# Four-layer graph network: comparisons moved to VectorE, and three steps reordered across the engine queues

## The chip, the cores and the metric

The kernel runs on one core of a Trainium2 chip. The metric is the device time of one execution in microseconds (us), here the median of several runs. A core has five engines that run side by side and meet through semaphores: PE (TensorE, matrix products), DVE (VectorE), ACT (ScalarE), POOL (GpSimd) and SP, which in this kernel issues nearly all of the DMA transfers. PEld is TensorE's weight load.

## What is computed

The input `x` is 32 x 512 x 128 (32 batches, 512 nodes, 128 features) and `adj` is 512 x 512, about one eighth of it non-zero. Four layers follow each other, each of the form `x = x + layer(relu(layernorm(x)))`:

```python
# layer 0: attention whose scores are table values placed at adj's non-zero entries in row-major order
m   = adj > 0
idx = cumsum(m.reshape(-1)) - 1                  # an index beyond the 256 entries takes the last
A   = softmax(where(m, e[0][idx], -9e15), axis=1)
out = (A * I) @ (h @ W[0]) + (A * (1 - I)) @ (h @ W[1]) + bias
# layer 1: Chebyshev hops over adj, one product with Theta1, relu
# layer 2: relu(h @ psi); weights adj * adj; a two-layer perceptron of the messages and h
# layer 3: tanh-limited attention masked by adj, then @ x @ v
```

Products are in float32; the kernel splits their operands into three parts ("high", "low", "mid") and adds three products where it needs the precision.

## The kernel before

**The order is the source's order.** The whole body lies in `tc.manual_schedule(...)`: on PE, DVE, ACT and POOL the instructions stand as the Python statements issue them, and DMA issues marked `keep_in_program_order` stand so on SP. Each engine takes its instructions in order, so one that waits holds back all behind it. Many helpers are Python generators: `go(steps, n)` advances one by n steps, `next(steps)` by one. That is how pieces of later work are placed between pieces of earlier work.

**Tiles.** The 32 batches are 16 pairs (`NQ`), and 512 nodes are 4 row blocks (`NT`). A pair's `h` (normalised and rectified) is 8 tiles of 128x128 made by ACT on L313. Its statistics are four DVE instructions `bn_stats` and then small operations that give `sh` and `rs`. For pairs 0, 1 and 2 these are POOL's (L233 to L237, `early_stats`); for later pairs ACT takes the root (L255), DVE the inverse (L257) and POOL the shift (L259, L260).

**Turned h.** The products need `h` with features on the partitions. Pairs 0 to 2 are turned by PE (L596, L331) and copied by ACT. All others go by memory (`turn_steps`): DVE transposes in 32x32 blocks into `hb` (L349), SP issues four writes (L356), then one read (L358) brings `hT` back. In layer 2 and later `turn_half` (L1101, L1107) and `fetch` (L1115) do the same.

**The opening of layer 0** builds the softmax matrix from `adj`.
1. `m`, its row counts and their running sums `incl` and `before` are formed.
2. For each row block t, `lt` (L554) compares a row of numbers with `incl`, and `of_row` (L555) marks which table entries lie in that row block. PE sums over them (`p_row`, `p_known`).
3. ACT and DVE copy `pgs`; PE forms `p_upto`; DVE compares and counts (L616), which gives each entry's column `col_of`.
4. `at_row` and `at_col` (L619, L620) mark rows and columns; `at_part` (L624) marks the column with one of three parts of the table's value, for two groups `kk` of 128 entries: six operations of 128x512.
5. `score_rows(t)` has PE add these up into `p_later` (L656) and `p_val` (L660); `softmax_rows(t)` is two DVE operations (L667, L669) and ACT's exponential (L670); `scaled_rows(t)` divides (row 0 on POOL, L678; others on ACT, L680) and POOL takes the diagonal out (L683, L684).
6. The rows are turned by PE (L485) and split by ACT and DVE into `att_high`, `att_low`, `att_mid` (L376 to L390), a half at a time.

`project_first(b)` makes the three parts of `g`, pair 0's product with W[1]: PE (L446), `g_high` (ACT L638 for b = 0, DVE L636 for b = 1), `g_low` (DVE, L640), `g_mid` (POOL, L641).

**The rounds of layer 0.** `first_sums()` handles pair 0 and prepares pairs 1 to 4; `round0(q)` handles pair q. A round of PE is 16 matmuls with the diagonal's operand `hd` (L796), 16 of the next pair's projection `p_g` (L446), and 48 with att and `g` (L803): high, low and mid parts for each half I. `diagonal_of(q, b)` makes `hd` on POOL (L731) from turned h; `bias(q)` adds the layer's bias to x on POOL (L453); `g_high`, `g_low` and `g_mid` are on ACT (L468), DVE (L470) and POOL (L474). DVE adds the sums to x (L811).

**Layer 1** is one generator, `layer1`, driven as `next_layer`: its first steps are interleaved with the last rounds of layer 0. `straighten(q)` (POOL, L936) reorders turned h into `hs`; `split_up` and `split_turned` form three parts of `h` and `hs` (ACT L412, POOL L413, DVE L414); `first` is the product with adj (`p_x1T`, L397), `weighed` the products with Theta1 (`p_w`, L962 and L964), `mix` the second product with adj (`p_l`, L983), whose sums DVE finishes (L987, L989) and to whose `hs` POOL adds the bias (L977).

**Layer 2** begins inside the last round of layer 1 by way of `more(step)`, with steps 5 to 8 after the four final `mix` calls. `split_hT(n)` splits turned h of batch n (POOL L1150 and L1151, DVE L1153), `opened(n)` makes the first products with it (`p_feat` L1163, `p_hidden` L1166).

The places that the change touches, in this order, are the loop with L554, the two `go(normal[0], ...)` beside the pgs copies, the loop with L624, the sequence from `project` to `transpose_rows`, the end of `first_sums`, the middle of `round0`, the head of `layer1`, steps 4 and 5 of `more`, and the loop at the end of the body.

Of the kernel before, what the change touches and what calls it, by code (L numbers as in the profile page):

```python
# [29 lines left out]
def kernel(  # L30
# [520 lines left out]
    pg = [bank(f"p_row_{i}").rearrange("p (j k) -> p j k", j=2) for i in range(NT // 2)]  # L551
    for t in range(NT):
        s = prep.tile([P, NE], F16, tag="lt", name=f"lt_{t}", bufs=2)
        (nc.gpsimd if t in (1, 2) else nc.vector).tensor_scalar(s, cols[:, :NE], incl[:, t : t + 1], None, OP.is_lt)  # L554
        nc.vector.scalar_tensor_tensor(of_row[:, t, :], cols[:, :NE], before[:, t : t + 1], s,  # L555
                                       OP.is_ge, OP.mult)
        for j in range(NT):
            nc.tensor.matmul(pg[j // 2][:, j % 2, :], m[:, t, blk(j)], of_row[:, t, :],
                             start=(t == 0 and j % 2 == 0), stop=(t == NT - 1), skip_group_check=True)
# [3 lines left out]
    for kk in range(NK):  # L563
        for t in range(NT):
            nc.tensor.matmul(pb[:, kk, :], of_row[:, t, blk(kk)], known[:, t, :],
                             start=(t == 0), stop=(t == NT - 1))
    go(normal[0], 1)
    pgs = prep.tile([P, NT, NE], F16, name="pgs")
    nc.scalar.copy(pgs[:, 0:2, :], pg[0])
    nc.vector.tensor_copy(pgs[:, 2:4, :], pg[1])  # L570
# [1 line left out]
    nc.vector.tensor_copy(row_of, pb[:, :, 1])  # L572
    rest = prep.tile([P, NK], F32, name="rest")
    nc.vector.tensor_sub(rest, rows[:, :NK], pb[:, :, 0])
    go(normal[0], NT - 1)

    elastn = prep.tile([P, 1], F32, name="elastn")
    nc.gpsimd.tensor_scalar(elastn, elast, -1.0, None, OP.mult)
# [41 lines left out]
        nc.vector.tensor_scalar(at_col[:, kk, :], cols, col_of[:, kk : kk + 1], -1.0, OP.is_equal, OP.mult)  # L620
    for kk in range(NK):
        for i in range(3):
            eng = nc.gpsimd if kk and i else nc.vector
            eng.tensor_scalar(at_part[:, i, kk, :], cols, col_of[:, kk : kk + 1],  # L624
                              parts[i][:, kk : kk + 1], OP.is_equal, OP.mult)
    copies = [None, nc.scalar.copy, nc.scalar.copy]
    turned = [q and pe_steps(h[q], f"hT0_{q}", hT[q], copies[q]) for q in range(3)]
    g_tiles(0)
# [14 lines left out]
    project = [[project_first(b) for b in range(2)], project_steps(1, hT[1])]  # L643
    next(project[0][0])
    go(normal[0])
    go(project[0][0])


    diag = prep.tile([P, NT, P], F32, name="diag")
# [35 lines left out]

    squares = turn_adj()
    score_rows(0)
    softmax_rows(0)
    score_rows(1)
    go(early[1], 1)  # L690
    turn_first(1)
# [9 lines left out]
    go(early[1], 1)  # L701
    next(project[0][1])
    softmax_rows(3, lambda: inverse(2))
    go(early[1])
    scaled_rows(2)
    next(project[0][1])
    inverse(3)
    scaled_rows(3)
    pt = [bank(f"p_attT_{j}") for j in range(NT)]
    transpose_rows(pt, att, 0)  # L710
    transpose_rows(pt, att, 1)
# [101 lines left out]
    def first_sums():  # L813


        adiag.append(region0.tile([P, N], F32, name="adiag", bufs=1))
        ps = opened_sums(0)
        mixed(0, 0, ps[0], 0, True)
        transpose_rows(pt, att, 2)
        transpose_rows(pt, att, 3)  # L820
        for j in range(NT):
            att_high(j, 1, True)
        go(normal[1])
        go(early[2])
        att_low(1)
        att_mid(1)
        mixed(0, 0, ps[0], 1, True)
        mixed(0, 0, ps[0], 2, True)
        p_adiag = bank("p_adiag")
        for t in range(NT):  # L830
            nc.tensor.matmul(p_adiag[:, blk(t)], ones, diag[:, t, :], start=True, stop=True)
        nc.scalar.copy(adiag[0], p_adiag)
        diagonal_of(0, 0)
        diagonal_of(0, 1)
        next(turned[1])
        mixed(0, 1, ps[1], 0, True)
        go(turned[1])
        next(project[1])
        mixed(0, 1, ps[1], 1, True)
        mixed(0, 1, ps[1], 2, True)  # L840
        go(project[1])
        go(normal[2])
        own_sums(0, ps, False)
        diagonal_of(1, 0)
        diagonal_of(1, 1)
        go(ln3, NT + 1)
        for I in range(2):
            added(0, I, ps[I])
        next(turned[2])
        go(turned[2])  # L850
        go(ln3)
        normalise(3)
        go(ahead[4], NT + 1)
        go(turn(3))
        go(ahead[4])
        bias(0)

    def round0(q):

        more = q + 1 < NQ  # L860
        nothing = iter(())
        both = stats_of_two(q - 1, q + 5) if q + 5 < NQ else stats_steps(q - 1, apart=True)
        ps = opened_sums(q)
        own_sums(q, ps, True)
        if q == 1:
            normalise(4)
            go(ahead[5])
        elif q + 3 < NQ:
            go(turn(q + 3))
        if q + 4 < NQ:  # L870
            h[q + 4] = normed_tile(q + 4)
            normal_of = normed_steps(q + 4, h[q + 4])
        else:
            normal_of = nothing
        if q > 1:
            go(normal_of, NT)
        go(both, NT)
        if q == NQ - 1:
            next(next_layer)
        if more:  # L880
            diagonal_of(q + 1, 0)
            diagonal_of(q + 1, 1)
            steps = projection(q + 1)
            next(steps)
            bias(q + 1)
            go(steps)
        if q + 5 >= NQ:
            go(both)
        if q == 1:
            go(turn(4))  # L890
        go(normal_of)
        if q >= 5:
            go(sums_ahead, 1)
        for part in range(3):
            mixed(q, 0, ps[0], part, False)
        go(both, NT + 1)
        added(q, 0, ps[0])
        go(both)
        if q in (3, 4):
            next(squares)  # L900
            next(squares)
        if q == 5:
            go(squares)
        for part in range(3):
            mixed(q, 1, ps[1], part, False)
        added(q, 1, ps[1])
        if q == NQ - 1:
            own[q] = stats_steps(q)
        if q % 2 and q // 2 + NQ // 4 < NQ // 2:
            loads(q // 2 + NQ // 4)  # L910

    def layer1(more, square):
# [80 lines left out]
        turn(0)  # L993
        normalised(1)
        yield
        pair = small_tile("th_high", F32R), small_tile("th_low", F32R)
        th_parts = pair[0][:, : 2 * D], pair[0][:, 2 * D :], pair[1][:, : 2 * D]
        fixed_parts(th[:, 0:2, :].rearrange("p k f -> p (k f)"), *th_parts)
        split_up(0, 0)
        turn(1)  # L1000
        split_up(0, 1)
        split_up(1, 0)
        normalised(2)
# [435 lines left out]
    def more(step):  # L1439

        if step == 0:
            chunk(2, 0)
            chunk(2, 1)
        elif step == 1:
            turn_half(2, 0)
        elif step == 2:
            turn_half(2, 1)
            fetch(2, 0)
            entering["weights"] = weights_of_2()
            next(entering["weights"])  # L1450
        elif step == "weights":
            go(entering["weights"])
        elif step == 3:
            entering["split"] = steps_of_split(0)
            next(entering["split"])
        elif step == 4:
            chunk(2, 2)
            chunk(2, 3)
            go(entering["split"])
        elif step == 5:  # L1460
            turn_half(2, 2)
            opened(0)
            turn_half(2, 3)
            fetch(2, 1)
            split_hT(1)
        elif step == 6:
            weighed_by_phi(0)
            chunk(2, 4)
        elif step == 7:
            turn_half(2, 4)  # L1470
            chunk(2, 5)
        elif step == 8:
            turn_half(2, 5)
            chunk(2, 6)
# [2 lines left out]
    first_sums()  # L1477
    bias(1)
    for q in range(1, NQ):
        if q == NQ - 2:  # L1480
            next(next_layer)
        round0(q)
    own_scope.close()
# [38 lines left out]
```

## Time and profile before

| | |
|---|---|
| median of 3 runs | 897.44 us (895.27 to 898.77) |
| the profiled execution | 897.51 us, of which 895.7 us are its span (first to last instruction) |
| busy, share of the span | PE 98%, PEld 86%, DVE 79%, POOL 69%, ACT 64% |
| mean granted TensorE clock | 0.994 |
| DMA moved | 103.90 MB, mean 116 GB/s |
| PE busy in 0 to 20, 20 to 40, 40 to 60 us | 13.59, 16.75, 17.06 us |
| PE busy in 80 to 100 and 100 to 120 us | 20.00 and 20.00 us |

Times inside the execution are counted from the start of its span. A row of the profile names the line of the source, the engine, the operation, output <- inputs, shapes and the number of instructions. "Idle before, releaser" is how long the engine stood idle ahead of that instruction and what ended the idleness. Idle time of an engine that nobody waits for costs nothing. L313 stands for `h` in layers 0 and 1, L1092 for it in layers 2 and 3.

### The profile page before, as it was taken

To read this page: it belongs to the slowest core of one execution; us is meant where nothing else is said; L and a number is where in the kernel's file an instruction comes from. 1 tells how busy PE (TensorE), PEld (TensorE's weight loads), DVE (VectorE), ACT (ScalarE), POOL (GpSimd) and SP (SyncE) were. 2 spreads that over 40 slices of the span, in tenths; PEclk is the share of its full clock that TensorE was granted. 3 is DMA by queue.
4 is the path that set the end of the run, shared out by engine and by line. 5 is a ranking of instruction groups with operands and counts; after the bars stand their busy time and mean duration, and the time that the engine had idled before them with its cause. 6 is when DMAs were issued, how large, how long until landed. Compare 5 with 4: busy or idle time off the path is not lost.

```text
span 895.7 us, 16285 instructions
## 1 busy us (share of the span) xinstructions
PE 874.1 (98%) x5519; PEld 773.2 (86%) x5520; DVE 703.9 (79%) x1424; ACT 574.9 (64%) x1278; POOL 617.7 (69%) x629
## 2 busy tenths in 40 slices
PE   6989999999999999999999999999999999999998
PEld 3789999997888888888878888888888889999987
DVE  6778787557778777797678888888779898988875
ACT  3675555246555556555666888885688878766774
POOL 7678888848578777666867557666376766676664
PEclk9989999999999999999999999999999999999999
DMA  9128663222231222213143345455345555555432
GB/s 259 27 71 236 189 185 100 70 71 72 82 106 48 71 71 68 74 48 95 48 142 95 95 119 141 126 157 165 110 139 152 150 146 152 143 153 147 127 104 83
DMA packets 107683, 103.90 MB, mean 116 GB/s; under 512 B 9552, under 2 KB 94160, under 8 KB 107600
## 3 DMA queue, kind: packets, MB, share of 16 engines
q1 hardware_dynamic: 107312, 102.34, 40.6%
q8 instruction: 44, 0.72, 0.3%
q10 hardware_dynamic: 288, 0.52, 0.2%
q14 instruction: 39, 0.32, 0.1%
HBM read 53.02 MB, written 49.81 MB: 115 GB/s over the span
## 4 chain that ended last, share of the span: by engine, by line
PE 87%; POOL 6%; ACT 2%; issue 1%; DVE 1%; DMA 1%; SPq 0%; POOLq 0%; ACTq 0%; DVEq 0%
PE p_av L1290 12%; PE p_hidden L1186 10%; PE p_l L803 9%; PE p_score L1268 9%; PE p_l L983 9%; PE p_x1T L397 9%; PE p_w L962 5%; PE p_l L446 3%; PE p_z L446 3%; PE p_l L796 3%; PE p_g L446 3%; PE p_w L964 3%; PE p_query L1222 2%; PE p_feat L1163 2%; PE p_hidden L1166 2%; PE p_hv L1234 2%
## 5 line engine op out<-in xcount | busy, mean ns | idle before, releaser
L1290 PEld LDWEIGHTS p_av<-hv,ex 128*128 128x128 f32 x1024 | 119.1, 191 | 4.0 <-POOL hv L1252 1.0
L1290 PE MATMUL p_av<-hv,ex 128*128 128x129 f32 x1024 | 119.7, 274 | 0.8 <-POOL hv L1252 0.6
L313 ACT ACTIVATE h<-x,sh,rs 128x128 f32<-128x128 f32 x256 | 103.3, 483 | 17.6 <-POOL sh L282 10.1
L427 POOL TENSOR_TENSOR key<-key 128x512 fp32r<-128x512 f32 x32 | 47.9, 1496 | 84.1 <-DVE key L426 58.2
L1263 DVE TENSOR_TENSOR ex<-ex,adjTx 128x512 f32<-128x512 f32 x64 | 80.4, 1259 | 31.1 <-ACT ex L1261 29.6
L1263 POOL TENSOR_TENSOR ex<-ex,adjTx 128x512 f32<-128x512 f32 x64 | 99.6, 1574 | 6.9 <-issue 3.5
L1092 ACT ACTIVATE h<-x,sh,rs 128x128 f32<-128x128 f32 x256 | 102.9, 484 | 0.0
L413 POOL TENSOR_TENSOR low_h<-h,high_h 128x512 fp32r<-128x512 f32 x32 | 55.6, 1739 | 44.9 <-PE p_w L964 32.5
L1269 ACT ACTIVATE ex<-p_score 128x512 f32<-128x512 f32 x128 | 76.3, 598 | 11.5 <-PE p_score L1268 4.7
L1261 ACT ACTIVATE ex<-ex 128x512 f32<-128x512 f32 x128 | 77.3, 634 | 0.0
L1150 POOL TENSOR_SCALAR high_hT<-hT 128x512 fp32r<-128x512 f32 x32 | 20.5, 642 | 57.4 <-PE p_hidden L1166 26.6
L246 DVE BATCH_NORM_STATS2 bn<-x 128x6 f32<-128x256 f32 x160 | 58.2, 418 | 0.0
L1206 POOL TENSOR_TENSOR x<-x,phi2b 128x256 f32<-128x256 f32 x64 | 55.7, 890 | 0.0
L413 POOL TENSOR_TENSOR low_hs<-hs,high_hs 128x512 fp32r<-128x512 f32 x32 | 44.1, 1388 | 15.7 <-ACT high_hs L412 15.3
L399 ACT COPY x1T<-p_x1T 128x512 f32<-128x512 f32 x32 | 18.7, 586 | 56.1 <-PE p_x1T L397 56.1
L1268 PE MATMUL p_score<-high_query,key 128*128 128x512 f32 x128 | 50.6, 395 | 0.0
L1268 PE MATMUL p_score<-low_query,key 128*128 128x512 f32 x128 | 50.5, 394 | 0.0
L1268 PE MATMUL p_score<-mid_query,key 128*128 128x512 f32 x128 | 50.4, 394 | 0.0
L431 ACT ACTIVATE high_query<-p_query 128x512 fp32r<-128x512 f32 x32 | 19.2, 601 | 47.5 <-PE p_query L1222 47.5
L964 PE MATMUL p_w<-th,x1T 128*128 128x128 f32 x256 | 49.0, 272 | 0.0
L962 PE MATMUL p_w<-th_high,high_hs 128*128 128x256 f32 x128 | 45.4, 355 | 0.1
L1151 POOL TENSOR_TENSOR low_hT<-hT,high_hT 128x512 fp32r<-128x512 f32 x32 | 42.5, 1328 | 4.3 <-POOL high_hT L1150 2.3
(249 smaller groups left out, 2619.5 us busy)
## 6 DMA issues: line engine op xcount, KB each, us to landing
d<-hb SPq DMA_DIRECT2D x128, 128.0 KB, 2.4
hT<-d SPq DMA_DIRECT2D x32, 512.0 KB, 3.7
d_hT<-hb_hT SPq DMA_DIRECT2D x116, 128.0 KB, 2.4
hT<-d_hT SPq DMA_DIRECT2D x29, 512.0 KB, 3.3
x<-in_x_dram SPq DMA_DIRECT2D x32, 256.0 KB, 5.1
dv<-hvb SPq DMA_DIRECT2D x128, 64.0 KB, 1.9
hvt<-dv SPq DMA_DIRECT2D x32, 256.0 KB, 2.7
out_dram<-x SPq DMA_DIRECT2D x31, 256.0 KB, 2.5
```

The lines of the kernel that those rows point to most:

```text
L313: nc.scalar.activation(h[:, b, t, :], xt[q][:, b, t, :], AF.Relu, bias=shift[q][:, i : i + 1], scale=scale[q][:, i : i + 1])
L397: nc.tensor.matmul(p, right[part][:, blk(t)], left[part][:, t, :], start=(t == 0 and part == 0), stop=(t == NT - 1 and part == 2))
L413: nc.gpsimd.tensor_sub(low, x, high.bitcast(F32))
L446: nc.tensor.matmul(p[:, blk(t)], hT(t), w, start=(i == 0), stop=(i == len(terms) - 1))
L803: nc.tensor.matmul(p[:, i * 2 * D : (i + 1) * 2 * D], att_parts[part][:, t, blk(2 * I + i)], g[q][part][:, t].rearrange("p b f -> p (b f)" ...
L962: nc.tensor.matmul(p, hs_parts[q, b][part][:, blk(t)], th_parts[part], start=(part == 0 and t % 2 == 0), stop=False, skip_group_check=True)
L983: nc.tensor.matmul(p, adj_parts[part][:, t, blk(i)], w[r][part][:, t, :], start=(part == 0 and t == 0), stop=(part == 2 and t == NT - 1))
L1092: nc.scalar.activation(h[:, t, :], xt[q][:, b, t, :], AF.Relu, bias=shift[q][:, i : i + 1], scale=scale[q][:, i : i + 1])
L1186: nc.tensor.matmul(sums2[n], weighed_features[n][i][:, blk(t)], sq[i][:, t, :], start=False, stop=(i == 2 and t == NT - 1), skip_group_che ...
L1263: eng.tensor_mul(split(ex[:, t, :]), split(ex[:, t, :]), crossed(mask[:, t, :]))
L1268: nc.tensor.matmul(p, keys[n][i][:, t, :], query[n][i], start=(i == 0), stop=(i == 2))
L1290: nc.tensor.matmul(po[:, i, : D + 1], ex[:, t, blk(i0 + i)], hv[:, t, :], start=(t == 0), stop=(t == NT - 1))
```

## The change

Five edits; no arithmetic is added or removed.

1. `lt` of row blocks 1 and 2 (L554) and `at_part` of group 1, parts 1 and 2 (L624), four instructions, go from POOL to DVE. Two of pair 0's h tiles, not one, stand ahead of ACT's pgs copy.
2. The second and third step of pair 0's `project_first(0)` stand after row 0's scores and softmax; on DVE this puts `g_low` behind row 0's two softmax operations.
3. The last steps of pair 1's early statistics (four POOL operations) stand after row 3's diagonal, not between the diagonals of rows 1 and 2.
4. `diagonal_of(2, ...)` (two POOL operations) is issued at the end of `first_sums`, ahead of `bias(0)` and `bias(1)`, not in round 1 behind them and pair 5's shift.
5. Layer 1's first two steps are each taken one or two rounds sooner: h of pair 0 in round 13, its transposes and transfers with h of pair 1 in round 14, and the transposes and transfers of pair 1 in round 15. In layer 2 the transposes of batches 2 and 3 and the read of their turned h come in step 4, before the last four `mix` calls, not in step 5.

```diff
-        (nc.gpsimd if t in (1, 2) else nc.vector).tensor_scalar(s, cols[:, :NE], incl[:, t : t + 1], None, OP.is_lt)
+        nc.vector.tensor_scalar(s, cols[:, :NE], incl[:, t : t + 1], None, OP.is_lt)
...
-    go(normal[0], 1)
+    go(normal[0], 2)
     pgs = prep.tile([P, NT, NE], F16, name="pgs")
...
-    go(normal[0], NT - 1)
+    go(normal[0], NT - 2)
...
         for i in range(3):
-            eng = nc.gpsimd if kk and i else nc.vector
-            eng.tensor_scalar(at_part[:, i, kk, :], cols, col_of[:, kk : kk + 1],
-                              parts[i][:, kk : kk + 1], OP.is_equal, OP.mult)
+            nc.vector.tensor_scalar(at_part[:, i, kk, :], cols, col_of[:, kk : kk + 1],
+                                    parts[i][:, kk : kk + 1], OP.is_equal, OP.mult)
...
     next(project[0][0])
     go(normal[0])
-    go(project[0][0])
...
     score_rows(0)
+    next(project[0][0])
     softmax_rows(0)
+    go(project[0][0])
     score_rows(1)
...
     softmax_rows(3, lambda: inverse(2))
-    go(early[1])
     scaled_rows(2)
     next(project[0][1])
     inverse(3)
     scaled_rows(3)
+    go(early[1])
     pt = [bank(f"p_attT_{j}") for j in range(NT)]
...
         go(ahead[4])
+        diagonal_of(2, 0)
+        diagonal_of(2, 1)
         bias(0)
...
-        if q == NQ - 1:
-            next(next_layer)
         if more:
-            diagonal_of(q + 1, 0)
-            diagonal_of(q + 1, 1)
+            if q > 1:
+                diagonal_of(q + 1, 0)
+                diagonal_of(q + 1, 1)
             steps = projection(q + 1)
...
         turn(0)
         normalised(1)
         yield
+        turn(1)
+        yield
         pair = small_tile("th_high", F32R), small_tile("th_low", F32R)
...
         split_up(0, 0)
-        turn(1)
         split_up(0, 1)
...
             go(entering["split"])
-        elif step == 5:
             turn_half(2, 2)
-            opened(0)
             turn_half(2, 3)
             fetch(2, 1)
+        elif step == 5:
+            opened(0)
             split_hT(1)
...
     for q in range(1, NQ):
-        if q == NQ - 2:
+        if q >= NQ - 3:
             next(next_layer)
         round0(q)
```

## The prediction

> **What bounds the kernel now.** I read the page first, then what TensorE waited for, then the time line of each engine where it waits. On the page, row PE is the busy share in 40 slices of 22.4 us, PEclk the granted clock.
>
> ```profile
> PE   6989999999999999999999999999999999999998
> PEclk9989999999999999999999999999999999999999
> ```
>
> From the fourth slice on PE is the bound, and only less PE work or a removed PE stall can shorten that part. The opening, to about 67 us, is not PE-bound: idle time, and one slice at reduced clock. TensorE's waits say where (total us, times, longest):
>
> ```profile
> PE p_l L796 <- POOL hd L731: 3.8, 2, 3.4
> PE p_val L660 <- POOL at_part L624: 3.2, 2, 1.7
> ...
> PE p_w L962 <- POOL low_hs L413: 1.7, 2, 1.5
> ...
> PE p_feat L1163 <- POOL low_hT L1151: 1.3, 1, 1.3
> ```
>
> POOL ends all four, and the change aims at just these. In the time lines (start, length):
>
> ```profile
> 17.67 4.56 POOL L624 TENSOR_SCALAR at_part<-cols,col_of,part 128x512 bf16<-128x512 f16 x2
> 32.09 1.67 POOL L236 TENSOR_TENSOR rs<-sd,minus_half 128x8 f32<-128x8 f32 x1
> 53.67 5.03 POOL L453 TENSOR_TENSOR x<-x,b 128x512 f32<-128x512 f32 x4
> 59.15 2.50 POOL L731 TENSOR_TENSOR hd<-hT,adiag 128x512 f32<-128x512 f32 x2
> 60.47 0.80 PE L796 MATMUL p_l<-w,hd 128*128 128x128 f32 x2 [3.41 <-POOL hd L731]
> 61.70 3.35 PE L796 MATMUL p_l<-w,hd 128*128 128x128 f32 x14 [0.43 <-POOL hd L731]
> ```
>
> See that hd of pair 2 stands behind 5.03 us of biases, and that 14 matmuls then take 3.35 us where sixteen take 1.95 elsewhere. The windows tell why (length, PE busy, clock, DMA):
>
> ```profile
> 57.00:60.40 3.40, 0.06 (x1) 1.00 0.48 154
> 60.40:63.80 3.40, 2.90 (x12) 0.50 0.33 74
> 63.80:67.20 3.40, 3.40 (x18) 0.50 0.30 85
> ```
>
> The stall is followed by 6.8 us at half clock.
>
> **The Trainium skill.** "TensorE: Matmul & The Clock Gate", section "What's actually happening": half rate after an idle window of about 3.4 us, full rate again after a busy one. The windows agree; 0.06 us busy of 3.4 was idle enough. "GPSIMD Engine Reference", section "4.1 Engine selection": elementwise work belongs on VectorE, though one-input operations run at roughly line rate on GpSimd. The trace is harsher: at_part takes 2281 ns on POOL and 407 on DVE, lt 966 and 278. "SBUF — State Buffer", section "SBUF: two separate sides": GpSimd and a VectorE operation with two SBUF inputs exclude each other. Partly so here: one of_row (L555) took 703 ns beside POOL's lt, the others 483 to 490.
>
> **Part 1, comparisons on DVE.** L554: DVE gains two of 278 ns, but it had waited 0.23 and 0.21 us for POOL's: even. POOL loses 1.92 us, so pair 0's first statistics, 10.35 to 12.68, can run from 8.3 to about 10.6 (port conflicts with of_row may cost either side up to 0.7, the range of this step). ACT now does two h tiles (0.41 each) before the pgs copy; both fit before p_row ends at 12.15, so the copy starts at 12.2, not 13.11. p_upto starts at 12.7, not 13.73; DVE's L616, behind its two bn (13.6), at 13.6, not 14.49: 0.9 earlier. L624: six at_part at a pitch of 0.33 on DVE, from 16.89 - 0.9 = 16.0 to 16.0 + 5 x 0.33 + 0.41 = 18.05. POOL delivered its second at 22.24. So p_val of row 0 ends at 18.5, not 22.66, and DVE's L669 starts at 18.6, not 22.69. DVE then bounds the softmax: TENSOR_TENSOR_REDUCE, g_low, one bn, u (0.62 + 0.61 + 0.34 + 0.66), then for row 1 0.62 + 0.07 + 0.67 + 0.66, for row 2 0.62 + 0.07 + 0.33 + 0.65 and an inverse of 0.1: 6.1 us, so row 3's L669 at 24.7, not 30.17. g_low of pair 0 (moved behind row 0's softmax) costs DVE nothing new. ACT's last exp and two scalings end at 27.5.
>
> **Part 2, pair 1's statistics behind row 3.** Four POOL operations, 31.59 to 34.04, 2.45 us. Without them between, row 3's diagonal ends at 29.0, not 35.95; they run 29.1 to 31.5. PE turns rows 2 and 3 by 29.75 and ends the low products at 30.7. What is late next: g_mid of pair 0 (L641, queued behind the statistics) ends at 32.85, so PE waits 2.2 us; and ACT's four h of pair 1 wait for 31.5 with att_high's second half queued behind them. ACT then needs 1.65 + 1.22 + 1.65 to 35.9, adiag 0.5, first turned copy 36.95; p_g of pair 1 starts at 37.0, not 41.21. **The opening gains 4.2 us.** Left in place, the statistics would end at 28.7 and row 3 at 30.65; I take the move alone as -1 to +1.
>
> **Part 3, pair 2's diagonals before the biases.** From p_g of pair 1 the chain is ACT in series (g_high, eight h, table load, sd, turned copies, eight h, sd, then DVE's rs and POOL's sh): sh of pair 4 at 53.72 - 4.2 = 49.5. hd of pair 2 at 49.5 + 2.5 = 52.0; PE ends pair 1's products at 57.06 - 4.2 = 52.85. No stall, no half clock. But three things come due:
> - Turned h of pair 3: DVE's transpose ends at 53.27, its read lands at 60.54; minus 4.2 that is 56.35. PE's own sums end at 54.65: it waits 1.7, then p_g to 58.2, high and low products to 60.1.
> - g_mid of pair 2: 52.0 + biases 5.0 + sh of pair 5 0.5 + bias 2 2.5 + 1.3 = 61.3. PE waits 1.25; the mid products start at 61.35, not 69.67: **8.3 us earlier**, the part before included.
> - Queued behind the biases as well: sh of pair 5 (57.5, was 59.19), eight h, DVE's statistics of pair 0 (they need bias 0, at 54.5), hd of pair 3 (64.4, needed at 65.2), turned h of pairs 4 and 5, which SP issues in order with the x loads (about 67.0 and 75.7; needed 67.0 and 76.4). The cover is thin: another 0 to 1.5 us.
> Later POOL needs 2.5 + 2.5 + 1.3 + 0.5 = 6.8 us a round against PE's 9.33, and recovers.
>
> **Part 4, layer 1.** ACT's eight h of pair 0 (3.18 us) move into round 13, where ACT idles 7.72 before L468; DVE's transposes (1.29 per pair) into the ends of rounds 13 and 14, into idle of over 2 us; eight writes and two reads go on an SP queue that is empty there. So hs (L936), held until 200.86 by the transfer, starts when POOL's low_h ends, 197.8. low_hs of both halves ends by 203; p_w needs the first at 202. The wait of 1.47 and 0.13 ahead of it go: 1.6 us. The waits of 0.16 and 0.23 further on stay.
>
> **Part 5, layer 2.** The second turned h waited at DVE (446.12) behind a sum that POOL's bias (L977) held until 445.05. ACT's h is ready at 441.95; transposed by 442.65, with the same 8.5 us to its landing (447.4 to 455.9), it is there at 451.2, not 456.04. The wait of 1.29 goes. The sum behind it starts 0.1 later, hidden by POOL's hs until 445.05.
>
> **Sum.** 8.3 + 1.6 + 1.3 = 11.2 us off the profiled execution (897.51; span 895.7 to 884.5), which lies 0.07 above the median of the runs shown (897.44): 886.2. If no stall in Part 3 came (bound from below), 3 us more: 883; with 0.7 of conflicts, 1 for Part 2, 1.5 of thin cover and half of Parts 4 and 5 lost, 891.
>
> **The rivals.**
> - *The feeders take part of it back* (0.24). One new PE idle stretch of 1.7 to 2.2 us meets the clock windows badly, one or two windows at half clock (1.7 us each), or the thin cover breaks. For it: three new stalls. Against: none is the 3.4 us of before, and the stretch 12.6 to 16.0 had PE busy only from 13.73 to 15.66 and full clock after it. 889 to 892.9.
> - *The opening's gain is handed back in rounds 2 to 5* (0.06). hd's wait only becomes a wait for turned h or g_mid of the same length, since neither transfers nor biases got shorter. Then Parts 4 and 5 remain: 897.4 - 2.9 = 894.5. Against: turned h lands 4.5 us before PE used it.
> - *Slower* (0.04). One mechanism: in rounds 1 to 3 PE, fed in pieces, falls to half clock again and again. A window of 3.41 us costs 1.7, so the 11.2 are gone from seven windows, 0.5% lost from ten: about 903. Against: at half clock PE needs 18.7 us a round, its feeders catch up, and full windows release it.
> - That the change doesn't act is excluded: the engines' instruction orders of the two kernels differ as the parts say.
>
> **How the numbers follow.** My forecast has 0.66: 882.5 to 889, most likely 886.2. With the first rival the range is 882 to 892. About 0.5%, 4.5 us, is what a measurement can tell from no change. Faster by more: 0.66 + 0.24 - 0.01 = 0.89; within: 0.06 + 0.01 = 0.07; slower: 0.04.
>
> **Right or wrong.** Right: no wait for at_part; L669 of row 0 near 18.6; p_g of pair 1 near 37; hd of pair 2 ready before PE; full clock from 52 to 68; no wait for low_hs of 1.5 nor for low_hT; POOL's third high_hT near 441 in the new time. Wrong: half clock after 52 us, a wait over 3 us for g_mid, hd or hT in rounds 2 to 5, a start of round 2's mid products later than 64.

## The result and the profile after

The changed kernel takes **886.18 us** (median of 4 runs, 885.88 to 886.49) against 896.49 (895.27 to 898.77, 4 runs) for the kernel before: a ratio of 0.9882, 95% interval 0.9860 to 0.9905. The forecast was 886.2. The profiled execution took 886.07 us with a span of 884.3, where the prediction had 884.5.

The two rows of the page, 40 slices of 22.1 us:

```profile
PE   8889999999999999999999999999999999999998
PEclk9999999999999999999999999999999999999999
```

The clock's 8 in the third slice is gone. What TensorE waited for, from the view of its waits (total us, times, longest), the main ones of layer 0 from 14 us on:

```profile
PE p_g L446 <- DMA hT<-d_hT: 1.7, 1, 1.7
PE p_attT L485 <- POOL att L682: 1.3, 1, 1.3
PE p_l L803 <- POOL g_mid L474: 1.0, 1, 1.0
PE p_attT L485 <- POOL sh L234: 0.7, 1, 0.7
...
PE p_g L446 <- DVE x L811: 0.5, 1, 0.5
PE p_l L803 <- POOL g_mid L640: 0.5, 1, 0.5
```

Of the four waits shown of before, those for hd, at_part and low_hT are gone and that for low_hs is down to 0.2. Two of the new ones (1.7 for turned h, 1.0 for g_mid) are those that the prediction named. The time lines of VectorE, GpSimd and TensorE at the places shown of before (start, length, and in brackets the idle time ahead with what ended it):

```profile
15.45 2.02 DVE L623 TENSOR_SCALAR at_part<-cols,col_of,part 128x512 bf16<-128x512 f16 x6
...
29.61 1.67 POOL L236 TENSOR_TENSOR rs<-sd,minus_half 128x8 f32<-128x8 f32 x1
...
49.48 2.54 POOL L731 TENSOR_TENSOR hd<-hT,adiag 128x512 f32<-128x512 f32 x2
51.98 4.98 POOL L453 TENSOR_TENSOR x<-x,b 128x512 f32<-128x512 f32 x4
...
52.72 1.95 PE L796 MATMUL p_l<-w,hd 128*128 128x128 f32 x16
56.33 2.02 PE L446 MATMUL p_g<-w,hT 128*128 128x128 f32 x16 [1.67 <-DMA hT<-d_hT]
...
61.23 1.21 PE L803 MATMUL p_l<-g_mid,att_mid 128*128 128x256 f32 x8 [0.96 <-POOL g_mid L474]
```

Six at_part take 2.02 us on VectorE, where two of them took 4.56 on GpSimd. hd of pair 2 now stands ahead of the biases, is ready at 52.02, and its sixteen matmuls take 1.95 us in one piece. The windows around them (length, PE busy with its number of matmuls, clock, DMA share, GB/s) show the clock at 1.00 throughout:

```profile
57.00:60.40 3.40, 3.27 (x29) 1.00 0.34 75
60.40:63.80 3.40, 2.58 (x21) 1.00 0.48 114
63.80:67.20 3.40, 3.40 (x32) 1.00 0.95 306
```

### The profile page after: what moved, and what is told of

Same layout as the page of the kernel before. It is cut to its first block, busy times and chain, and to the rows that moved or that the text cites. A ratio compares the mean times of both kernels' runs of the same rounds, so it can differ in the third digit from the quotient of the medians.

```text
span 884.3 us, 16285 instructions
## 1 busy us (share of the span) xinstructions
PE 869.4 (98%) x5520; PEld 769.9 (87%) x5520; DVE 704.2 (80%) x1428; ACT 574.3 (65%) x1278; POOL 610.8 (69%) x625
## 4 chain that ended last, share of the span: by engine, by line
PE 89%; DVE 4%; POOL 3%; ACT 2%; issue 1%; DMA 0%; POOLq 0%; DVEq 0%; ACTq 0%
PE p_av L1292 13%; PE p_l L984 10%; PE p_hidden L1188 10%; PE p_x1T L397 10%; PE p_score L1270 9%; PE p_l L803 8%; PE p_w L963 5%; PE p_l L446 3%; PE p_z L446 3%; PE p_w L965 3%; PE p_g L446 3%; PE p_feat L1165 3%; PE p_hidden L1168 3%; PE p_l L796 2%; PE p_query L1224 2%; PE p_hv L1236 2%
## 5 line engine op out<-in xcount | busy, mean ns | idle before, releaser
L1152 POOL TENSOR_SCALAR high_hT<-hT 128x512 fp32r<-128x512 f32 x32 | 20.5, 642 | 56.0 <-PE p_hidden L1168 28.8
L414 DVE SCALAR_TENSOR_TENSOR mid_h<-h,high_h 128x512 fp32r<-128x512 f32 x32 | 28.1, 883 | 23.8 <-ACT high_h L412 15.1
L432 DVE SCALAR_TENSOR_TENSOR z<-p_z,z 128x512 fp32r<-128x512 f32 x31 | 21.4, 690 | 30.9 <-ACT z L431 30.9
```

## The experiments

Where a part is undone (u1 to u5), or more is changed (u6 and the labels with i), the comparison is with the changed kernel's 886.18; where a part stands alone (labels with p), with the kernel before in the same set of runs. The changed kernel was timed in one set only. The kernel before, timed in all four, has medians of 896.49 there, 896.14 beside u1, u2, u3 and p3, 895.70 beside u4, u5, u6 and i2, and 897.48 beside p1, i3, i4 and i5. So a difference between medians of two sets can be off by 1 us or more. By the ratios to the kernel before, u1 is 4.5 us later than the changed kernel, u3 3.9, u4 3.8 and u5 2.1, i5 is 3.0 sooner, and u2, u6 and i2 differ from it by about 0.5 or less.

Runs of one kernel differ in their mean granted clock, and that number is needed to read them. In the traces the clock is either full or half, and each stretch at half clock after the start is 3.41 or 6.83 us long, one or two windows. By that length one window costs up to 1.7 us, where TensorE is the bound, and takes 0.0019 off the mean over some 890 us.

**u1: Part 1 undone, the rest kept.** Not shown: the order of pair 0's h tiles and of its g steps goes back too (the first and second of the five edits).

```diff
-        nc.vector.tensor_scalar(s, cols[:, :NE], incl[:, t : t + 1], None, OP.is_lt)
+        (nc.gpsimd if t in (1, 2) else nc.vector).tensor_scalar(s, cols[:, :NE], incl[:, t : t + 1], None, OP.is_lt)
...
-            nc.vector.tensor_scalar(at_part[:, i, kk, :], cols, col_of[:, kk : kk + 1],
-                                    parts[i][:, kk : kk + 1], OP.is_equal, OP.mult)
+            eng = nc.gpsimd if kk and i else nc.vector
+            eng.tensor_scalar(at_part[:, i, kk, :], cols, col_of[:, kk : kk + 1],
+                              parts[i][:, kk : kk + 1], OP.is_equal, OP.mult)
```

> The changed kernel with Part 1 alone undone: two lt and two at_part comparisons back on GpSimd, the pair-0 statistics and g_low in their old places; the other four parts stay. Theory A, Part 1 carries the opening and Part 2's move only keeps its place: at_part ends near 22.2 us again, p_val of row 0 near 22.5, the mid products of pair 0 about 4.7 us later than in the changed kernel, and the end about 5.3 us later: 891.5. Theory B, the statistics' move carries a part by itself (row 3's diagonal is 1.6 us earlier whatever the comparisons do): the end only about 2.6 us later, 888.8. Should the idle PE ahead of 22 us meet a clock window, half clock near 23 to 26 us adds up to 1.7 to either.

890.18 us (889.01 to 892.04), ratio to before 0.9932 (0.9917 to 0.9947): 4.0 later. TensorE's time line in u1:

```profile
19.80 0.38 PE L660 MATMUL p_val<-at_part,at_row 128*128 128x512 bf16 x1 [1.43 <-POOL at_part L624]
21.86 0.38 PE L660 MATMUL p_val<-at_part,at_row 128*128 128x512 bf16 x1 [1.69 <-POOL at_part L624]
```

Row 0's p_val ends at 22.24 instead of 17.90. The mid products of pair 0 start 4.04 later than in the changed kernel (36.89), p_g of pair 1 3.56 later, p_g of pair 5 2.91 later: the earlier kernel runs into the wait for turned h of pair 5 (0.48 us), which u1 doesn't. The size lies between the theories, and p_g of pair 1 at 40.59 is only 0.3 sooner than before (41.21, less the 0.32 by which the adjacency matrix arrived later in that execution). With the comparisons on GpSimd the other order of the statistics gives next to nothing, which speaks against theory B. Half clock doesn't hide a gain here: u1 has a window of it at 33.6 to 37.0, which slows the mid products, but p_g follows ACT and comes 5.60 us after its first h of pair 1, against 5.44 in the changed kernel. The kernel before has its own window, at 22.8 to 26.2.

**p1: Part 1 alone, on the kernel before.** The edit is u1's whole edit read from plus to minus.

> The kernel before with Part 1 alone: all lt and at_part comparisons on VectorE, pair 0's statistics ahead of the sums; statistics of pair 1, pair 2's diagonals and layers 1 and 2 as before. Theory A, the opening's chain (ACT, then POOL's sh and hd) is carried whole to the end: p_g of pair 1 about 4 us sooner, hd's wait of 3.4 us stays with its half clock, the end 4.0 us less than before, 892.0. Theory B, the earlier opening only lengthens the wait at hd of pair 2, whose biases hold it: under 1 us less. Theory C, besides the chain the half-clock window at 22.8 to 26.2 us goes for good: up to 5.7 us less, 890.4.

892.84 us (891.09 to 894.00) against 897.48, ratio 0.9950 (0.9934 to 0.9966): 4.6 less. The time line of TensorE in p1:

```profile
36.65 1.95 PE L446 MATMUL p_g<-w,hT 128*128 128x128 f32 x16
...
55.88 0.80 PE L796 MATMUL p_l<-w,hd 128*128 128x128 f32 x2 [3.39 <-POOL hd L731]
57.10 3.36 PE L796 MATMUL p_l<-w,hd 128*128 128x128 f32 x14 [0.42 <-POOL hd L731]
```

p_g of pair 1 starts 4.56 us sooner than before, and the wait for hd with its half clock is there unchanged, 4.6 us sooner as a whole. That is nearest to theory A: the opening is one chain, and Part 1 alone carries all of its gain to the end.

**u2: pair 1's statistics ahead of row 2's diagonal again.**

```diff
     softmax_rows(3, lambda: inverse(2))
+    go(early[1])
     scaled_rows(2)
     ...
     scaled_rows(3)
-    go(early[1])
```

> The changed kernel with the move of Part 2 alone undone: pair 1's statistics on GpSimd stand ahead of row 2's diagonal again, not behind row 3's. Theory A, ACT is the chain there and its four h of pair 1 only wait for these statistics: they end 2.4 us sooner, h of pair 1 starts sooner, p_g of pair 1 near 36.0 instead of 37.0, and the end about 1.0 us sooner, 885.2. Theory B, row 3's diagonal is the chain: it ends 1.6 us later (30.65 instead of 29.03), rows 2 and 3 are turned later, and the end is 1.6 us later, 887.8. My prediction put this move at -1 to +1.

885.67 us (884.94 to 886.16), ratio 0.9880 (0.9864 to 0.9896): 0.5 sooner, within what the runs scatter. ACT's first h of pair 1, first in u2 and then in the changed kernel:

```profile
28.93 1.65 ACT L313 ACTIVATE h<-x,sh,rs 128x128 f32<-128x128 f32 x4 [0.57 <-POOL sh L237]
```

```profile
31.59 1.65 ACT L313 ACTIVATE h<-x,sh,rs 128x128 f32<-128x128 f32 x4 [3.43 <-POOL sh L237]
```

The move made ACT wait 2.7 us longer, and what it bought, row 3's diagonal at 29.03 instead of 30.79, bought no time: the end is not later without it, so theory B falls. In u2's profile the clock was at half from 30.6 to 34.0, so that its p_g of pair 1 (37.51) can't be set against 37.03. i3 below can: up to there it is u2 with four transposes repeated, its first comparison starts at the same time as the changed kernel's (4.38 and 4.37), and neither has half clock in the opening.

```profile
35.91 1.95 PE L446 MATMUL p_g<-w,hT 128*128 128x128 f32 x16
```

That is theory A's 36.0, 1.1 us sooner than 37.03. How much of it reaches the end isn't shown: 0.5 by the medians, no more than the scatter.

**u3: pair 2's diagonals behind the biases again.**

```diff
-        diagonal_of(2, 0)
-        diagonal_of(2, 1)
         bias(0)
...
-            if q > 1:
-                diagonal_of(q + 1, 0)
-                diagonal_of(q + 1, 1)
+            diagonal_of(q + 1, 0)
+            diagonal_of(q + 1, 1)
```

> The changed kernel with Part 3 alone undone: pair 2's diagonals on GpSimd stand behind the two biases again. hd of pair 2 is ready near 57.5 instead of 52.0, and PE, done with pair 1's products at 52.75, waits for it. Theory A, the wait costs about its length and is followed by no half clock, or most of it would have gone into the next waits (turned h of pair 3 at 56.35, g_mid of pair 2 at 61.2) anyway: 1 to 1.5 us later, 887.4. Theory B, the idle stretch meets a clock window and PE runs at half clock for 3.4 to 6.8 us behind it as in the kernel before: 4 to 5 us later, 890.5.

889.76 us (888.52 to 890.22), ratio 0.9925 (0.9912 to 0.9938): 3.6 later. TensorE's time line and windows in u3:

```profile
57.41 0.80 PE L796 MATMUL p_l<-w,hd 128*128 128x128 f32 x2 [3.40 <-POOL hd L731]
58.64 3.35 PE L796 MATMUL p_l<-w,hd 128*128 128x128 f32 x14 [0.43 <-POOL hd L731]
61.78 2.53 PE L446 MATMUL p_g<-w,hT 128*128 128x128 f32 x16
```

```profile
57.00:60.40 3.40, 2.56 (x10) 0.50 0.25 59
60.40:63.80 3.40, 3.40 (x21) 0.62 0.38 100
```

The mid products of pair 2 start at 66.07, 4.84 later; 1.14 of that is there at p_g of pair 1 already, from half clock at 28.9 to 35.7 in u3's opening. Of the other 3.70, waiting is 1.2 (3.40 and 0.43 here, against 1.67 and 0.96 in the changed kernel), as theory A had it; the rest, 2.5, is the sixteen matmuls and p_g at half clock. Theory B is nearer: most of what Part 3 is worth at this place is the clock.

**p3: Part 3 alone, on the kernel before** (u3's edit read the other way).

> The kernel before with Part 3 alone: pair 2's diagonals on GpSimd ahead of the biases, everything else as before. Theory A, as the prediction's sum has it (8.3 less the opening's 4.2, less what the new waits for turned h and g_mid take): the wait of 3.4 us and the half clock behind it go, but PE then waits for turned h of pair 3 and g_mid of pair 2: 3.6 us less than before, 892.9. Theory B, nothing new comes due: wait and half clock go whole, 7.3 us less, 889.2. Theory C, the wait for g_mid and turned h takes the place of the one removed: under 1 us less.

894.33 us (892.30 to 896.14, 17 runs) against 896.14 (22 runs), ratio 0.9973 (0.9963 to 0.9983): 1.8 less. The profiled run, 892.93, is where theory A has it; its waits are 1.7 for turned h of pair 3 and 0.9 for g_mid, so there theories B and C fall. The median lies between A and C, and the clock goes with it. With one exception, 892.93, the 17 times form three groups: clock 0.997 or 0.998, 892.3 to 892.8; 0.996, 894.1 to 894.7; 0.994, 895.2 to 896.1. By their size, each step is one more window at half clock. The profiled run has two, at 13.9 and at 34.4. The first lies where TensorE still waits for at_part and the like (length, PE busy, clock):

```profile
12.60:16.00 3.40, 2.38 (x11) 0.69 0.96 279
16.00:19.40 3.40, 3.11 (x19) 0.81 1.03 287
```

In its trace the kernel before lost two windows behind the wait for hd and one in the opening, and most of its runs have the same mean clock. Why so many runs of p3 have two or three without that wait is open: to about 50 us the two kernels run the same instructions.

**u4: layer 1's turned pairs late again.** The edit is the layer-1 part of the change undone: `turn(1)` between the two `split_up` calls, the extra yield taken out, `next(next_layer)` back in round0 and in one outer round only.

> The changed kernel with Part 4 alone undone: h, transposes and transfers of layer 1's first two turned pairs in their old places. Theory A, the wait for low_hs is the whole price and comes back as it was in the trace of before, with the 0.13 beside it: 1.6 us later, 887.8. Theory B, the part gave what the start times of p_w differ by in the two traces (from 7.95 us ahead at layer 1's first p_w to 9.7 ahead behind it, and 0.3 before it): 2.0 us later, 888.2. Theory C, the wait is hidden because the kernel is earlier there by itself: no difference.

888.80 us (888.71 to 890.47), ratio 0.9924 (0.9912 to 0.9937): 2.6 later, more than any theory. TensorE's time line from the first p_w to the first with x1T, and a window, in u4; then the same time line in the changed kernel:

```profile
193.93 0.38 PE L965 MATMUL p_w<-th_high,high_hs 128*128 128x256 f32 x1
195.78 0.39 PE L965 MATMUL p_w<-th_high,low_hs 128*128 128x256 f32 x1 [1.47 <-POOL low_hs L413]
...
196.12 0.39 PE L967 MATMUL p_w<-th,x1T 128*128 128x128 f32 x2
```

```profile
196.00:200.00 4.00, 4.00 (x23) 0.59 0.10 38
```

```profile
194.23 0.28 PE L963 MATMUL p_w<-th_high,high_hs 128*128 128x256 f32 x1
...
194.59 0.39 PE L965 MATMUL p_w<-th,x1T 128*128 128x128 f32 x2
```

The wait is back, 1.47 as in the kernel before, and from the first p_w to p_w's first products with x1T pass 2.19 us as before, 0.36 in the changed kernel: 1.83, and 2.0 with the gap ahead of the first p_w (counted from the last x1T products ahead of it). Behind it the clock falls for one window, about 0.41 x 4 us = 1.6. In the profile of before the same wait had full clock behind it. So the part is worth 2 us in waiting and up to 1.6 more, by whether the stall meets a window.

**u5: layer 2's second turned h late again.**

```diff
             go(entering["split"])
-            turn_half(2, 2)
-            turn_half(2, 3)
-            fetch(2, 1)
         elif step == 5:
+            turn_half(2, 2)
             opened(0)
+            turn_half(2, 3)
+            fetch(2, 1)
             split_hT(1)
```

> The changed kernel with Part 5 alone undone: the second turned h of layer 2 behind the sum that waits for GpSimd's bias. Theory A, the wait of 1.29 us ahead of p_feat comes back and is the whole price: 1.3 us later, 887.5. Theory B, as the two traces differ around p_feat (from 9.7 us ahead to 11.3): 1.6 us later, 887.8. Theory C, nothing comes back, since POOL's queue is earlier there: 886.2.

887.33 us (886.64 to 888.05), ratio 0.9905 (0.9892 to 0.9919): 1.1 later by the medians, 2.1 by the ratios, 0.6 in the profiled run. But the wait for low_hT did not come back. SP's queue, first in the kernel before, then in u5:

```profile
447.45 1.75 SPq L1107 DMA_DIRECT2D d<-hb  x4
452.65 0.34 SPq L1115 DMA_DIRECT2D hT<-d  x1
```

```profile
436.95 1.75 SPq L1109 DMA_DIRECT2D d<-hb  x4
440.73 0.34 SPq L1117 DMA_DIRECT2D hT<-d  x1
...
461.98 1.75 SPq L1109 DMA_DIRECT2D d<-hb  x4
467.59 0.34 SPq L1117 DMA_DIRECT2D hT<-d  x1
```

From the first write to the read pass 5.2 us in the kernel before and 3.8 in u5. The last write was issued 3.9 us ahead of the read in the one, 2.45 in the other. In the kernel before the DMA view shows the last 1.5 us of it at 7 to 27 GB/s, so one write seems to have straggled (p1 and p3, with 3.9 each, show the same). In u5 the straggler is a later pair, at 461.98, where nothing waits for it. In the kernel before, the straggling is by itself long enough for the wait: 1.4 us of lateness against 1.29. Part of that wait was also GpSimd's low_hT, which took 1.77 us there, beside VectorE's mid_hT, and takes 1.3 in the changed kernel. The 0.6 us that u5's profiled run did lose has another cause, VectorE's mid_hT, which starts together with one of GpSimd's bias operations (L978). In u5, then in the changed kernel, then in u6, which follows:

```profile
430.28 1.84 DVE L1155 SCALAR_TENSOR_TENSOR mid_hT<-hT,high_hT 128x512 fp32r<-128x512 f32 x1
430.27 1.30 POOL L978 TENSOR_TENSOR hs<-hs,b 128x512 f32<-128x512 f32 x1
```

```profile
430.79 0.68 DVE L1155 SCALAR_TENSOR_TENSOR mid_hT<-hT,high_hT 128x512 fp32r<-128x512 f32 x1
430.79 1.83 POOL L978 TENSOR_TENSOR hs<-hs,b 128x512 f32<-128x512 f32 x1
```

```profile
430.26 1.85 DVE L1155 SCALAR_TENSOR_TENSOR mid_hT<-hT,high_hT 128x512 fp32r<-128x512 f32 x1
430.27 1.29 POOL L978 TENSOR_TENSOR hs<-hs,b 128x512 f32<-128x512 f32 x1
```

In each, one of the two runs in its usual time (0.68 or 1.3) and the other ends about 0.55 us after it. In u5 and u6 it was VectorE's that came second, and TensorE waited 0.72 and 0.84 for it; in the changed kernel it was GpSimd's, and TensorE didn't wait. The recorded starts don't say which goes first: in u5 GpSimd's is 0.01 us ahead, in u6 VectorE's. Theory C is nearest for the wait, none for the time; what makes a write straggle is open.

**u6: the x loads behind the turned h on SP.**

```diff
         elif q + 3 < NQ:
             go(turn(q + 3))
+        if q % 2 == 0 and (q - 1) // 2 + NQ // 4 < NQ // 2:
+            loads((q - 1) // 2 + NQ // 4)
...
-        if q % 2 and q // 2 + NQ // 4 < NQ // 2:
-            loads(q // 2 + NQ // 4)
```

> The changed kernel with the x loads of rounds 1, 3, 5 and 7 issued at the start of the next round, behind the writes and the read of the turned h on SP, not ahead of them. Theory A, these loads are why turned h of pair 5 lands late (its read is issued 5.4 us after its last write; 2.0 us for pair 4): the read goes out near 69 us instead of 72.87, the wait of 0.5 us before p_g of pair 5 goes, and the end comes 0.5 to 0.6 us sooner, 885.6. Theory B, the landing is bound by what writes the turned h, not by the loads: the read stays near 72.9 and the end at 886.2. If the x loads then come too late for layer 0's tail, the end is later than 886.2.

885.97 us (885.40 to 886.51), ratio 0.9888 (0.9875 to 0.9902): no difference that these runs can tell. Locally theory A is right. SP's queue in the changed kernel and in u6:

```profile
62.48 2.08 SPq L135 DMA_DIRECT2D x<-in_x_dram  x4
64.61 2.86 SPq L356 DMA_DIRECT2D d_hT<-hb_hT  x4
72.87 0.34 SPq L358 DMA_DIRECT2D hT<-d_hT  x1
```

```profile
62.97 2.08 SPq L356 DMA_DIRECT2D d_hT<-hb_hT  x4
67.34 0.34 SPq L358 DMA_DIRECT2D hT<-d_hT  x1
67.73 2.08 SPq L135 DMA_DIRECT2D x<-in_x_dram  x4
```

The read goes out 5.5 us sooner, the wait is gone, and p_g of pair 5 starts at 76.28 instead of 76.92. The view had put that wait down to VectorE's x (L811); in u6 this ends at 76.86 as before, and p_g doesn't wait for it: it was the transfer. But the wait needs no edit to go: in u2, u4 and u5, with the loads in their old place, the read is issued at 72.19, 72.19 and 71.86, and p_g of pair 5 starts at 76.73, 76.46 and 76.47 without a wait. So the changed kernel's 0.48 is scatter of transfers against a thin cover, and there was little for u6 to gain. Its 0.64 us is lost again in layer 2, at the slow mid_hT shown above.

**i2, i3, i4, i5: the next waits.** i2 takes u2's order and u6's loads, transposes h of pair 4 ahead of the statistics that wait for bias 0, puts g_mid of pair 2 ahead of bias 2, and the high products of pair 2 ahead of p_g of pair 3 (`ahead_of(q)` is 1 for q = 2 and else 0; u2's and u6's edits, shown above, are left out):

```diff
             go(ahead[5])
+            go(turn(4))
...
+            for part in range(ahead_of(q)):
+                mixed(q, 0, ps[0], part, False)
             steps = projection(q + 1)
             next(steps)
-            bias(q + 1)
+            if q > 1:
+                bias(q + 1)
             go(steps)
+            if q == 1:
+                bias(2)
...
-        if q == 1:
-            go(turn(4))
...
-        for part in range(3):
+        for part in range(ahead_of(q), 3):
```

> The changed kernel with the next waits of its opening attacked together: pair 1's statistics ahead of row 2's diagonal again, turned h of pair 4 (ready on ACT at 52.75, transposed at 57.0) transposed ahead of the statistics that wait for bias 0, g_mid of pair 2 ahead of bias 2 on GpSimd, the high products of pair 2 ahead of p_g of pair 3 (cover for its turned h), and the x loads behind the turned h on SP. Theory A, these waits (1.7 for turned h of pair 3, 1.0 for g_mid of pair 2, 0.5 for turned h of pair 5) are separate and come off to the part that hd of pair 3 (ready at 64.2) leaves: mid products of pair 2 near 59.4 instead of 61.2, own sums of pair 3 near 63.8 instead of 65.2, the end 1.9 us sooner, 884.3. Theory B, one common chain feeds them all and only moves: under 0.5 us, 885.9.

885.24 us (883.14 to 886.43), ratio 0.9878 (0.9861 to 0.9894). The times scatter by clock: 883.14 at a clock of 1.0, the others at 0.995 and 0.996. The wait for g_mid is gone, that for turned h of pair 3 is 0.8 instead of 1.7, and a new one of 0.73 for hd of pair 3 follows. The run at full clock is beyond theory A, the median is nearer to B. In the profiled run the clock was at half from 28.8 to 35.6, and p_g of pair 1 started at 38.15, against 35.91 in i3; TensorE, that much later, has less to wait for turned h, so the 0.8 isn't the edit's alone.

i3 is i2 with one line more, `transpose_rows(pt, att, 0)` done twice, to keep TensorE busier there:

> The kernel i2 with row 0's four transposes done twice, the second time in PE's idle time ahead of row 1's (1.25 us); the values written are the same. Theory A, i2's opening runs at half clock for 3.4 to 6.8 us near 28 to 35 us because PE is thinly busy before, and the added 0.66 us of work keeps the clock up: mean clock 0.998 or more in most runs and the median near i2's undisturbed run, 883.2 to 884. Theory B, the window needs more than this: clock 0.996 as in i2, 885.2.

884.98 us (884.66 to 886.83), ratio 0.9866 (0.9847 to 0.9885). Four of five runs have a clock of 0.998, which is more even than i2, but the median is no better. Neither theory is shown. Its profile has no half clock near 28 us, p_g of pair 1 starts 1.1 us sooner than in the changed kernel, and the gain is gone again at p_g of pair 3 (56.91 against 56.33), after a wait of 2.4 for its turned h. The read of this h went out at 51.95 and p_g started 5.0 us later, where the changed kernel has 53.05 and 3.3; in i3 the writes of pair 4 go out 1.3 us behind that read. i4 and i5 have 4.6 and 4.3, but i2, in the same order, 3.3. That the writes slow the read is likely, not shown.

i4 is i2 with hd of pair 3 ahead of the statistics, bias 2 cut in halves around it:

```diff
-                bias(2)
+                bias_half(2, 0)
+                diagonal_of(3, 0)
+                diagonal_of(3, 1)
...
         go(both)
+        if q == 1:
+            bias_half(2, 1)
```

> The kernel i2 with hd of pair 3 on GpSimd ahead of the statistics of pairs 0 and 6 and between the halves of bias 2. Theory A, PE's wait of 0.73 us for hd of pair 3 was the last one in the first rounds and goes: 0.7 us less than i2 at equal clock, median 884.5, 882.4 without half clock. Theory B, the later statistics and second half of bias 2 hold VectorE and the turned h of pair 5 instead: no gain or a loss of up to 1 us.

884.33 us (882.10 to 886.42), ratio 0.9854 (0.9832 to 0.9876); at a clock of 0.999, 882.10. Theory A: the wait for hd is gone. 

i5 is i4 with the statistics behind row 3's diagonal, as in the changed kernel:

> The kernel i4 with pair 1's statistics behind row 3's diagonal, as in the changed kernel. Theory A, that order costs about 0.5 us at equal clock but PE's half clock near 30 to 35 us is rarer in it: the same as i4 within 0.5 us. Theory B, the order is worth 1 us one way: 883.5 or 885.5 against 884.5.

**883.68 us** (883.11 to 884.92), ratio 0.9849 (0.9831 to 0.9868). All four runs lie below the four of the changed kernel, so this is the best median here, 2.5 us below; the two ratios' intervals overlap a little. Against i4 it is neither theory: 0.65 lower in the median, but 1.0 higher in the best run. TensorE's longest wait in i5, after the start, is still for turned h of pair 3:

```profile
PE p_g L446 <- DMA hT<-d_hT: 1.7, 1, 1.7
```

## Why the prediction was right

| step | predicted | measured |
|---|---|---|
| pair 0's first statistics end | 10.6 | 10.31 |
| six at_part on VectorE | 16.0 to 18.05 | 15.45 to 17.47 |
| L667 or L669 of row 0, row 3 | 18.6, 24.7 | 18.28, 24.85 |
| row 3's diagonal, statistics of pair 1 end | 29.0, 31.5 | 29.03, 31.55 |
| low products of pair 0 end | 30.7 | 32.37 |
| wait for g_mid of pair 0 | 2.2 | 0.48 |
| p_g of pair 1 starts | 37.0 | 37.03 |
| hd of pair 2 ready | 52.0 | 52.02 |
| waits for turned h of pair 3, g_mid of pair 2 | 1.7, 1.25 | 1.67, 0.96 |
| mid products of pair 2 start | 61.35 | 61.23 |
| Part 4 | 1.6 | 2.1 between the traces, 2.6 if undone |
| Part 5 | 1.3 | 1.57 between the traces, 1.1 if undone |

The close agreement is in part luck. The adjacency matrix arrived 0.32 us sooner in the changed kernel's profiled execution than in that of before (VectorE's first comparison starts at 4.37, not 4.69), which no part of the change does; without it the start times to 61.23 would each be about that much later. And the runs of the kernel before spread over 3.5 us: the gain is 10.3 us by the medians, 11.4 between the profiled runs, against 11.2 predicted.

**Part 1** was right, and its weight was underrated: p1 shows that it alone carries the whole gain of the opening, 4.6 us. That hd's wait moves with the chain instead of taking the gain up (the rival "handed back") is p1's other result.

**Part 2** had its range right, -1 to +1: the move costs about 1 us at p_g of pair 1 (i3), and nothing or some 0.5 us at the end (u2). One term inside was mis-sized: rows 2 and 3 were to be turned by 29.75, but ran from 29.76 to 31.42. They wait bank by bank for VectorE's att_mid (L390, 29.20 to 30.60), which reads the banks that they overwrite; the prediction priced the transposes alone. This cause is read from the trace; no run tested it. The trace of before could have told the length, since the same eight transposes take the same time there. Before, then after:

```profile
35.07 1.67 PE L485 MATMUL p_attT<-ident,att 128*128 128x128 f32 x8 [0.68 <-POOL att L684]
```

```profile
29.76 1.67 PE L485 MATMUL p_attT<-ident,att 128*128 128x128 f32 x8 [0.69 <-POOL sh L234]
```
The slip cost nothing, since g_mid, due at 32.85, ended the next wait anyway: the 2.2 us became 0.48 of waiting and 1.7 of slower turning.

**Part 3** held in each number. u3 ends 3.6 us later by the medians; at the mid products of pair 2 the part is worth 3.7, of which only 1.2 is waiting. The thin cover broke at one place, turned h of pair 5, for 0.48 us, and only in some executions (u2, u4 and u5 have no such wait). The prediction named the x loads on SP and had 0.7 us of margin there (75.7 against 76.4).

**Part 4** was under-sized: the 1.47 and 0.13 of idle time leave out the slow restart and the matmuls that then come one by one, 2.1 in all, and where the stall meets a clock window, as in u4, 1.6 more.

**Part 5** has its size right and its cause half wrong. The wait that it was to remove needed both the late transpose and a straggling write, and the step took the 8.5 us from transpose to landing for a constant. With the order undone and no straggler the wait stays away in u5's trace; yet u5 is later in all its runs than any run of the changed kernel, for a reason that is shown only in its profiled run.

**The rivals.** Half clock repeated did not come: mean clock 0.996 to 0.999 in the four runs, where the kernel before has 0.994 in most. That difference, about 0.0033 of 890 us, is some 3 of the 10.3 us: the clock gave time here, where the first rival feared that it would take some, and Part 3's 8.3 had counted this. But the argument against that rival was too strong. It said that none of the new stalls is long enough, and the full clock of the profiled run seems to bear it out. u3 and u6 run the same instructions to about 50 us, and both fell to half clock, at 28.9 and 28.5 us for 6.8 and 3.4 us, with no wait over 1.3 us in the 14 us ahead. It cost 1.1 us at p_g of pair 1 in u3 and nothing at the mid products of pair 2 in u6. So the profiled run was lucky in its windows, at a small price.

## What to carry to other kernels

Follow one chain of start times to the place where two waits meet, and let the later one decide; that made the sum right though a term inside it was off by 1.7 us. A stall's price has three terms: the idle time, the slow restart behind it, and the clock; the last is a matter of where the window falls, so look at the mean clock of each run before a part's worth is told from its median. A part that acts through the clock is lost from sight when runs of equal clock are compared: at 0.994, p3 takes 895.2 to 896.1 us, the kernel before in the same set 894.8 to 897.8. Undo each part by itself: of the five here one gave nothing that the times can tell, and one removed a wait that stayed away without it in the one trace kept.

## What the runs showed of the hardware that was not expected

- A GpSimd bias and a VectorE operation with two SBUF inputs that started within 0.01 us of each other took turns whole: VectorE's 0.68 us became 1.84 (u5) or 1.85 (u6), or GpSimd's 1.31 became 1.83 (changed kernel). The order of the recorded starts did not tell which. The prediction had found the exclusion only "partly so" from an of_row of 703 ns. "SBUF — State Buffer", section "SBUF: two separate sides", of the Trainium skill has it as an exclusion, and here the trace agrees.
- From the last of four equal writes' issue to the read that depends on them passed 3.9 us instead of 2.45 in three traces (before, p1, p3) at the same transfer; in u5 it was a later transfer. Why is open.
- Half clock did not need a wholly idle window. In the fourteen traces here it began 17 times between the start and the end of TensorE's work. TensorE had been busy for 0.04 to 2.58 of the 3.41 us ahead of it, and in eleven of these for 1.8 or more; u4's wait of 1.47 us was enough. Stretches as thin kept full clock elsewhere: 2.17 and 2.49 of 3.40 us between 22.8 and 29.6 in the changed kernel.
- Runs of one kernel differ in the number of windows at half clock: p3's times differ by up to 3.8 us, in steps of about 1.7.
